# The last job of a four-layer network at its end: gate first, rotations on VectorE, shorter Newton steps, delivery tile by tile

## The chip, the cores and the metric

The kernel runs on one core of a Trainium2 chip, in one launch. The metric is the device time of that launch in microseconds (us). In this document PE is TensorE (PEld its weight loads), DVE is VectorE, ACT is ScalarE, POOL is GpSimd and SP is SyncE, which issues the DMAs. Each engine works through its own queue of instructions in order, and engines wait for each other by semaphores.

## What is computed

Input `x` has shape (4, 512, 256): B = 4 batch rows, S = 512 positions, D = 256 features, all fp32. Four layers follow each other, each added to `x` after a normalisation over the features:

```
x = x + attention_a(layernorm(x))       # 16 heads, full projections, causal softmax
x = x + gated(layernorm(x))
x = x + attention_b(layernorm(x))       # low-rank attention with rotary positions
x = x + gated(layernorm(x))
```

The change touches the gated layer alone. Its sequence axis is the batch axis: batch row l attends to rows m <= l, and each of the 512 positions is by itself. Cut to what matters:

```
x      = silu(x_prev * conv_w[:, 0] + x * conv_w[:, 1])   # x_prev: the former batch row
q      = silu(x @ Wq);  k = x @ Wk;  v = x @ Wv;  g = x @ Wg
q, k   = rotary(q), rotary(k)                             # by the batch row's number
onehot = one of two choices per head, by the larger of v @ router_w; score = its softmax value
norm   = 1 / (number of rows m <= l with the same choice)
a[m]   = (q . k[m]) * score * norm where the choices agree, times HDK**-0.5
o      = sum over m <= l of a[m] * v[m]
o      = (o - mean) / sqrt(var + eps) per head            # 16 heads of 16 numbers
out    = (silu(g) * o) @ Wout
```

## The kernel before

**Tiles and stages.** A batch row lies in four tiles `x[b][t]` of 128 positions by 256 features. The matmuls need the features on the partitions, so `norm` normalises a tile into `xn` and PE transposes it, by way of PSUM (`ps_tp`), into `xT`; even tiles are copied out by DVE, odd ones by ACT (L225). `gated` (L607 to L820) handles half of a batch row, two tiles, in one job; there are 16 jobs (two layers, four rows, two halves). It is a generator: a list of work lanes steps it, one `yield` at a time, between the pieces of the attention layers.

**The order of the work.** Nothing is rescheduled: the order in which the program emits instructions is the order of each engine's queue. During both attention layers strings of letters (`BESIDE_FULL`, `BESIDE_LOWRANK`) say which lane is stepped next: `n` the norms, `a` and `b` the two places of the gated jobs. When these strings are used up, a loop steps `"nab"` until nothing is left. Then two jobs are still open: the one before the last (row 2, second half), which has its output product and its additions to `x` ahead of it, and the last norm (row 3, second half), which hands over to the last gated job. Nothing runs beside the last job.

**One gated job, in the order of its lines.**
- Convolution: POOL multiplies the present position's `xT` with the second weight into `cx` (L619, two chunks of features); DVE adds the former row's `xT_before` times the first weight (L625). ACT takes a tanh (L630) and DVE forms the silu from it (L632); the weights hold the factor of a half.
- Projections (L641): for each of the two tiles a matmul group of 512 columns (q, k, v) and one of 272 (gate, and the difference of the two router scores `dl`). ACT copies them out of PSUM to `q`, `kv`, `gd` (L651, L652, L649).
- ACT: tanh of q (L685), of the gate (L699), of the score (`gap`, L707). DVE: choice `r` (L691), `gap` (L694), agreement `e` (L700), the silu of q (L705), `count` (L712), weights (L715 to L717), silu of the gate (L721), weights times agreement (L724).
- Rotations: `rotate` on POOL, for k and then q: four products of 128 columns (L671) and two sums (L675, L676) each.
- DVE: four products of q with the k of rows 0 to 3 and their sums per head (L734, L735), times the weights (L739).
- Weighing of the values: rows 0 and 3 by DVE, 1 and 2 by POOL (L749), with sums on DVE (L763, L769).
- ACT squares (L774); DVE sums to the variance (L777, L778) and makes a first guess of its inverse root by integer arithmetic (L783); POOL prepares `half_var` (L786) and multiplies `o` with the gate (L787); three Newton rounds of four small operations follow (L790 to L793), on POOL, in the last job on DVE.
- DVE multiplies with the root (L795), PE transposes all four blocks (L801), ACT copies them at once (L804), PE multiplies with `w_out` (L809), DVE adds to `x` (L816) tile by tile, and SP stores the tile (L1412).

**Dummy transposes.** `keep_going(count, a)` issues `count` PE transposes into a PSUM tile that nobody reads (L132), as soon as `a` is written. The last job has two such groups: 24 behind the transposes of the last norm and 70 behind L739.

In the last norm (`short`), POOL makes `rstd` by a power (L199, L200) and DVE forms both `xn` in one operation each (L211).

Of the kernel before, what the change touches and what calls it, by code (L numbers as in the profile page):

```python
# [13 lines left out]
AF = mybir.ActivationFunctionType  # L14
ALU = mybir.AluOpType
# [4 lines left out]
P = 128  # L20
# [46 lines left out]
def network(ctx: ExitStack, tc: tile.TileContext, ins: dict, out: bass.AP):  # L67
# [471 lines left out]
    def wide(tag, half, name=None, cols=None):  # L539
        tile_ = gpool.tile([P, gslots[tag]], F32, tag=f"{tag}_{half}", name=name or tag)  # L540
        return tile_[:, : cols or gslots[tag]]
# [65 lines left out]
    def gated(layer, l, xT, xT_before, half, after, newton, last=False):  # L607
# [9 lines left out]
        cx = wide("cx", half, "cx", DC * nt * P).rearrange("p (c s) -> p c s", c=DC)  # L617
        for c in range(DC):
            nc.gpsimd.tensor_scalar(  # L619
                cx[:, c, :], xT[:, c, rows], conv[:, c, 1:2], 1.0, ALU.mult, ALU.mult  # L620
            )
        yield
        if l:
            for c in range(DC):
                nc.vector.scalar_tensor_tensor(  # L625
                    cx[:, c, :], xT_before[:, c, rows], conv[:, c, 0:1], cx[:, c, :], ALU.mult, ALU.add
                )
            yield
# [8 lines left out]
        for i in range(nt):  # L637
            for lo, hi in ((0, 512), (512, NIN)):
                ps = ps_mm()
                for c in range(DC):  # L640
                    nc.tensor.matmul(  # L641
                        ps[:, : hi - lo],
                        lhsT=cx[:, c, i * P : (i + 1) * P],
                        rhs=w_in[:, c, lo:hi],
                        start=(c == 0),
                        stop=(c == DC - 1),
                    )
                if lo:
                    nc.scalar.copy(gd[:, i, :], ps[:, : DV + H])  # L649
                else:  # L650
                    nc.scalar.copy(q[:, i, :], ps[:, :DK])  # L651
                    nc.scalar.copy(kv[:, i, :], ps[:, DK:])  # L652
                yield
        gate, dl = gd[:, :, :DV], gd[:, :, DV:]
        turn_tmp = wide("cx", half, "turn")

# [22 lines left out]
        turn_k = rotate(kv[:, :, :DK]) if l else iter(())  # L679

        w0 = wide("w0", half, "thq")
        thq = w0[:, : nt * DK].rearrange("p (t k) -> p t k", t=nt)
        e = w0[:, HT * DK :][:, : B * nt * H].rearrange("p (m n) -> p m n", m=B)
        thg = wide("w1", half, "thg", nt * DV).rearrange("p (t v) -> p t v", t=nt)
        nc.scalar.activation(thq, q, AF.Tanh, scale=0.5)  # L685


        if l == 0:
            choices[half] = gpool.tile([P, B, HT * H], F32, tag=f"r_{half}", name="r")
        r = choices[half][:, l]  # L690
        nc.vector.tensor_scalar(r.rearrange("p (t h) -> p t h", t=nt), dl, -(2.0**-25), None, ALU.is_ge)  # L691
        history[layer, l, half] = kv
        gap = little("gap", nt * H)
        nc.vector.scalar_tensor_tensor(  # L694
            gap.rearrange("p (t h) -> p t h", t=nt), dl, -1.0, dl, ALU.mult, ALU.max
        )
        next(turn_k, None)
        yield
        nc.scalar.activation(thg, gate, AF.Tanh, scale=0.5)  # L699
        nc.vector.tensor_tensor(  # L700
            e[:, : l + 1], choices[half][:, : l + 1], r.unsqueeze(1).to_broadcast([P, l + 1, nt * H]), ALU.is_equal
        )
        next(turn_k, None)
        yield
        nc.vector.scalar_tensor_tensor(q, thq, 1.0, q, ALU.add, ALU.mult)  # L705

        nc.scalar.activation(gap, gap, AF.Tanh, scale=0.5)  # L707
        next(turn_k, None)
        yield
        count = little("count", nt * H)  # L710
        if l:
            nc.vector.tensor_reduce(count, e[:, : l + 1].rearrange("p m h -> p h m"), AX.X, ALU.add)  # L712
        else:
            nc.vector.tensor_copy(count, e[:, 0])
        nc.vector.reciprocal(count, count)  # L715
        nc.vector.tensor_scalar(gap, gap, 1.0, HDK**-0.5 / 4, ALU.add, ALU.mult)
        nc.vector.tensor_tensor(gap, gap, count, ALU.mult)  # L717
        turn_q = rotate(q) if l else iter(())
        next(turn_q, None)
        yield  # L720
        nc.vector.scalar_tensor_tensor(gate, thg, 1.0, gate, ALU.add, ALU.mult)  # L721
        next(turn_q, None)
        yield
        nc.vector.tensor_tensor(  # L724
            e[:, : l + 1], e[:, : l + 1], gap.unsqueeze(1).to_broadcast([P, l + 1, nt * H]), ALU.mult
        )
        next(turn_q, None)
        yield
# [11 lines left out]
        if last:  # L740
            keep_going(70, a_tile.rearrange("p m n -> p (m n)"))
# [13 lines left out]

        weigh(nc.vector, o, 0)
        if l:
            weigh(nc.gpsimd, part[1], 1)
        yield
        if l > 1:  # L760
            weigh(nc.gpsimd, part[2], 2)
# [12 lines left out]
        nc.scalar.activation(sq, og, AF.Square)  # L774
        yield
# [9 lines left out]
        )  # L785
        nc.gpsimd.tensor_scalar(half_var, var, -0.5, 1.0, ALU.mult, ALU.mult)  # L786
        nc.gpsimd.tensor_tensor(o, o, gate, ALU.mult)  # L787
        yield
        for _ in range(3):
            newton.tensor_tensor(square, root, root, ALU.mult)  # L790
            newton.tensor_tensor(square, square, half_var, ALU.mult)
            newton.tensor_scalar(square, square, 1.0, 1.5, ALU.mult, ALU.add)
            newton.tensor_tensor(root, root, square, ALU.mult)  # L793
            yield
# [11 lines left out]
        for i, t in enumerate(tiles):  # L806
            po = ps_mm()
            for c in range(DC):
                nc.tensor.matmul(  # L809
                    po[:, :D],  # L810
                    lhsT=oT[:, i, c * P : (c + 1) * P],
                    rhs=w_out[:, c, :],
                    start=(c == 0),
                    stop=(c == DC - 1),
                )
            nc.vector.tensor_tensor(x[l][t], x[l][t], po[:, :D], ALU.add)  # L816
            if after:
                after(l, t)
            yield
# [539 lines left out]
    def gated_half(layer, l, half, after=None, newton=nc.gpsimd, last=False):  # L1359

        xT = gated_in[layer][l]

        def job():
            yield from gated(layer, l, xT, gated_in[layer].get(l - 1), half, after, newton, last)
            if half:
                yield from finished(layer, l)

        return job(), half
# [10 lines left out]
    def then_gated_half(l, half):  # L1379


        def take(xT):
            gated_in[1][l] = xT

            last = (l, half) == (B - 1, 1)
            work.add(gated_half(1, l, half, store, nc.vector if last else nc.gpsimd, last))
            if last:
                keep_going(24, ident)

        short = (l, half) == (B - 1, 1)  # L1390
        return norm(l, take, tiles=HALVES[half], xT=gated_in[1].get(l), short=short)
# [23 lines left out]
    loop(attention_full(during_full, prologue))  # L1415
    while norms.jobs or work.jobs:
        beside("nab")
# [81 lines left out]
```

## Time and profile before

| | |
|---|---|
| runs, us | 1372.25, 1374.01, 1379.89; median 1374.01 |
| profiled execution, us | 1376.38 |
| its span, first to last instruction, us | 1374.7 |
| mean granted TensorE clock | 0.981 |
| instructions | 17452 |
| busy: PE, DVE, ACT, POOL | 95%, 58%, 46%, 42% of the span |
| last gated job, from the first xn to the last store issued | 1335.93 to 1372.40 us |

Times in the trace are microseconds from the start of the span. A busy share is an average over all stages; the chain of work that ended last follows the work back from the last instruction, at each step to what released it, and names engine and line. "Issue" in it is time for which the profile shows no cause. The granted clock is the share of full speed that TensorE's throttle allowed.

### The profile page before, as it was taken

The page shows a single profiled execution, that of the slowest core. Times are in us where ns is not written, and L with a number is a line of the kernel's source. Part 1 is how long each engine was busy: PE and PEld are TensorE (multiplying, and loading weights), DVE is VectorE, ACT ScalarE, POOL GpSimd, SP SyncE. Part 2 cuts the span into 40 slices and gives each one's busy share as a digit, 9 for nine tenths or more (in the row PEclk, how much of TensorE's full clock was granted, in tenths as well). Part 3 has the DMA queues.
Part 4 walks back from the last instruction along what each step waited for, and adds up shares of the span by engine and source line. Part 5 has one row for each costly group of instructions (what it writes and reads, how often), then busy time and mean ns, then how long its engine had stood idle before and what let it go on. Part 6 is the DMA issues. An engine that isn't in the chain of part 4 may idle for free.

```text
span 1374.7 us, 17452 instructions
## 1 busy us (share of the span) xinstructions
PE 1310.8 (95%) x5240; PEld 801.8 (58%) x5240; DVE 791.0 (58%) x2388; ACT 632.6 (46%) x1712; POOL 575.3 (42%) x1129
## 2 busy tenths in 40 slices
PE   9999999999999999999999888979899999999985
PEld 5555555555556656565555565647565666655554
DVE  4654445553665555755548655864646546565655
ACT  3433333343333343333343247554757666676631
POOL 3212212321125224331224745774547757675552
PEclk9999999999999999999999999989999998999998
DMA  3777765554555553554535410000000000000000
GB/s 116 223 230 213 218 201 175 161 161 123 161 167 155 161 161 108 161 165 147 164 103 176 138 32 0 1 1 1 1 9 4 5 9 1 9 1 8 1 16 8
DMA packets 88141, 133.83 MB, mean 97 GB/s; under 512 B 16112, under 2 KB 69872, under 8 KB 88048
## 3 DMA queue, kind: packets, MB, share of 16 engines
q1 hardware_dynamic: 88048, 132.72, 32.8%
q8 instruction: 42, 0.69, 0.2%
q14 instruction: 51, 0.42, 0.1%
HBM read 86.29 MB, written 46.40 MB: 97 GB/s over the span
## 4 chain that ended last, share of the span: by engine, by line
PE 80%; DVE 6%; POOL 6%; ACT 4%; issue 2%; DMA 1%; SPq 0%; POOLq 0%; DVEq 0%; ACTq 0%
PE ps_mm L338 16%; PE ps_sc L364 10%; PE ps_pz L426 10%; PE ps_mm L325 8%; PE ps_mm L448 8%; PE ps_mm L641 6%; PE ps_sc L1110 6%; PE ps_tp L1146 4%; PE ps_pz L1166 4%; PE ps_mm L1184 3%; PE ps_mm L809 2%; POOL probs L1138 1%; PE ps_mm L1084 1%; DVE ps_sc L1118 1%; ACT probs L1121 1%
## 5 line engine op out<-in xcount | busy, mean ns | idle before, releaser
L390 POOL TENSOR_SCALAR probs<-probs,sums 128x128 f32<-128x128 f32 (+3 forms) x256 | 135.8, 549 | 489.8 <-DVE sums L387 454.4
L375 ACT ACTIVATE probs<-ps_sc,sums 128x128 f32<-128x128 f32 (+3 forms) x256 | 135.0, 528 | 264.0 <-DVE sums L372 263.3
L1118 DVE CUSTOM_DVE_ANT_0 ps_sc<-ps_sc,mask_b 128x96 f32<-128x96 f32 (+15 forms) x256 | 112.3, 448 | 98.4 <-PE ps_sc L1110 90.0
L1138 POOL TENSOR_SCALAR probs<-probs,sums 128x160 f32<-128x160 f32 (+3 forms) x224 | 120.5, 556 | 111.6 <-DVE sums L1135 84.4
L1110 PE MATMUL ps_sc<-kTb,qTb 128*128 128x32 f32 (+15 forms) x512 | 159.3, 421 | 3.4 <-ACT probs L1121 3.2
L364 PE MATMUL ps_sc<-kT,qT 128*128 128x128 f32 (+3 forms) x512 | 159.2, 433 | 0.0
L1121 ACT ACTIVATE probs<-ps_sc,sums 128x160 f32<-128x160 f32 (+3 forms) x224 | 114.4, 512 | 97.0 <-DVE sums L1118 76.9
L372 DVE CUSTOM_DVE_ANT_0 ps_sc<-ps_sc,mask_a 128x128 f32<-128x128 f32 (+3 forms) x256 | 126.9, 499 | 45.7 <-PE ps_sc L364 44.8
L426 PE MATMUL ps_pz<-probsT,v 128*128 128x512 f32 (+3 forms) x512 | 148.7, 433 | 1.3 <-DMA probsT<-way 1.3
L426 PEld LDWEIGHTS ps_pz<-probsT,v 128*128 128x128 f32 x512 | 96.6, 190 | 77.8 <-issue 54.0
L439 DVE TENSOR_SCALAR zT<-ps_pz,bias 128x512 f32<-128x512 f32 x64 | 48.1, 751 | 149.1 <-PE ps_pz L426 149.0
L448 PE MATMUL ps_mm<-wo,zT 128*128 128x256 f32 x512 | 121.1, 380 | 1.3 <-ACT qTb L1018 1.3
L338 PE MATMUL ps_mm<-xT,wk 128*128 128x512 f32 x256 | 120.6, 593 | 0.4 <-ACT wvo L933 0.3
L338 PE MATMUL ps_mm<-xT,wq 128*128 128x512 f32 x256 | 120.4, 593 | 0.5 <-ACT xT L225 0.5
L325 PE MATMUL ps_mm<-wv,xT 128*128 128x512 f32 x256 | 120.3, 593 | 0.3 <-DVE xT L225 0.3
L399 DVE STREAM_TRANSPOSE squares<-probs 128x512 f32<-128x512 f32 (+3 forms) x256 | 115.1, 488 | 0.0
L1151 ACT COPY probsT<-ps_tp 128x512 f32<-128x512 f32 x160 | 92.9, 586 | 46.2 <-PE ps_tp L1146 44.7
L1146 PE MATMUL ps_tp<-ident,probs 128*128 128x128 f32 x608 | 99.7, 287 | 9.0 <-ACT probsT L1151 2.6
L364 PEld LDWEIGHTS ps_sc<-kT,qT 128*128 128x128 f32 x512 | 86.6, 191 | 34.5 <-issue 26.8
L332 ACT COPY v<-ps_mm 128x512 f32<-128x512 f32 x64 | 37.5, 586 | 148.1 <-PE ps_mm L325 148.1
L1146 PEld LDWEIGHTS ps_tp<-ident,probs 128*128 128x128 f32 x608 | 72.4, 144 | 56.2 <-issue 24.3
L448 PEld LDWEIGHTS ps_mm<-wo,zT 128*128 128x128 f32 x512 | 94.2, 191 | 18.5 <-issue 5.5
(159 smaller groups left out, 2066.4 us busy)
## 6 DMA issues: line engine op xcount, KB each, us to landing
way<-squares SPq DMA_DIRECT2D x64, 640.0 KB, 2.9
probsT<-way SPq DMA_DIRECT2D x256, 160.0 KB, 3.3
wv<-in_a_wv_dram SPq DMA_DIRECT2D x16, 512.0 KB, 5.0
wq<-in_a_wq_dram SPq DMA_DIRECT2D x32, 256.0 KB, 4.0
wk<-in_a_wk_dram SPq DMA_DIRECT2D x32, 256.0 KB, 3.9
wo<-in_a_wo_dram SPq DMA_DIRECT2D x16, 512.0 KB, 4.8
x<-in_x_dram SPq DMA_DIRECT2D x16, 128.0 KB, 3.9
out_dram<-x SPq DMA_DIRECT2D x16, 128.0 KB, 1.7
```

The costliest lines, as they stand in the source:

```text
L325: nc.tensor.matmul(pv, lhsT=xTs[b][:, c, t * P : (t + 1) * P], rhs=wv[g][:, c, :], start=(c == 0), stop=(c == DC - 1),)
L338: nc.tensor.matmul(ps, lhsT=w[u // 2][:, c, (u % 2) * DH : (u % 2 + 1) * DH], rhs=xTs[b][:, c, :], start=(c == 0), stop=(c == DC - 1),)
L364: nc.tensor.matmul(ps[:, :m], lhsT=queries[u][:, t * P : (t + 1) * P], rhs=keys[u][:, :m], start=True, stop=True,)
L372: nc.vector.tensor_tensor_reduce(ps[:, :m], ps[:, :m], mask[:, S - m :], -1.0, 3.0e38, ALU.add, ALU.min, nmax[:, t : t + 1])
L375: nc.scalar.activation(pr[:, t, :m], ps[:, :m], AF.Exp, bias=nmax[:, t : t + 1], scale=-1.0, accum_out=total[:, t : t + 1],)
L390: nc.gpsimd.tensor_scalar(pr[:, t, :m], pr[:, t, :m], inv[:, t : t + 1], 1.0, ALU.mult, ALU.mult)
L426: nc.tensor.matmul(z[:, :, k:, :], lhsT=v[:, k, j * DH : (j + 1) * DH], rhs=pT[:, :, f : f + m, :], start=(k == 0), stop=(k == NT - 1),)
L448: nc.tensor.matmul(po[:, :D], lhsT=zTs[HG * g + i][:, t].rearrange("p i b -> p (i b)"), rhs=wo[g][:, i, :], start=(i == 0), stop=(i == HG ...
L1110: nc.tensor.matmul(ps, lhsT=q[:, t % 2 * 4 + i].rearrange("p h q -> p (h q)"), rhs=kT[:, :m], start=True, stop=True,)
L1121: nc.scalar.activation(probs[i][:, :m], ps, AF.Exp, bias=nmax[:, i : i + 1], scale=-1.0, accum_out=total[:, i : i + 1],)
L1138: nc.gpsimd.tensor_scalar(probs[i][:, :m], probs[i][:, :m], inv[:, i : i + 1], 1.0, ALU.mult, ALU.mult)
L1146: nc.tensor.transpose(pt.rearrange("p (h i q) -> p h i q", h=4, i=4)[:, :, i, :], lw["probs"][t][s][i][:, k * P : (k + 1) * P], ident,)
```

## The change

It has six parts. The first two and the fourth also stand in other jobs' code, but only the first changes what they do.

1. Convolution: for rows after the first, POOL multiplies the *former* row's `xT_before` with the first weight, and DVE adds the present row. In all jobs with l > 0.
2. Behind the attention loop a line steps the lanes by `"nnnnnaaaaann"` before the `"nab"` loop starts. On the queues this has one effect: DVE's two `xn` of the last norm stand ahead of the two additions to `x` (row 2, second half), not behind them.
3. Last job only, gate first: both 272-column groups come ahead of both 512-column groups; all that depends on the gate columns alone is emitted between them; ACT takes the tanh of q tile by tile, each ahead of the copy of `kv`.
4. Last job only, rotations by DVE (`rotate_at_once`): per tensor two products of 256 columns and two sums of 128, q first, then k. The weighing of rows 1 and 2 and the product with the gate move to DVE too; the latter (`gated_o`) stands under ACT's square. POOL has no work in the last job after the convolution.
5. Last job only, Newton rounds of three operations: square, `(var * -0.5) * square`, `(square + 1.5) * root`; no `half_var`.
6. Last job only, the end tile by tile: root product, transposes and copy for 256 columns at a time. The dummy groups shrink from 24 to 18 and from 70 to 58.

The diff, cut:

```diff
-    def gated(layer, l, xT, xT_before, half, after, newton, last=False):
+    def gated(layer, l, xT, xT_before, half, after, last=False):
...
+        early, tap = (xT_before, 0) if l else (xT, 1)
         for c in range(DC):
             nc.gpsimd.tensor_scalar(
-                cx[:, c, :], xT[:, c, rows], conv[:, c, 1:2], 1.0, ALU.mult, ALU.mult
+                cx[:, c, :], early[:, c, rows], conv[:, c, tap : tap + 1], 1.0, ALU.mult, ALU.mult
             )
...
-                    cx[:, c, :], xT_before[:, c, rows], conv[:, c, 0:1], cx[:, c, :], ALU.mult, ALU.add
+                    cx[:, c, :], xT[:, c, rows], conv[:, c, 1:2], cx[:, c, :], ALU.mult, ALU.add
...
+                nc.scalar.copy(q[:, i, :], ps[:, :DK])
+                if last:
+                    nc.scalar.activation(thq[:, i, :], q[:, i, :], AF.Tanh, scale=0.5)
+                nc.scalar.copy(kv[:, i, :], ps[:, DK:])
...
+        if last:
+            parts.sort(key=lambda part: -part[1])
+            for part in parts[:nt]:
+                project(*part)
+            later = parts[nt:]
...
+        def rotate_at_once(a):
+            pairs = a.rearrange("p t (n j) -> p t n j", j=HDK // 2)
+            shape = [P, nt, 2 * H, HDK // 2]
...
+            for i in range(2):
+                nc.vector.tensor_tensor(
+                    tmp[i], pairs, rot[:, i, l - 1, :].unsqueeze(1).unsqueeze(1).to_broadcast(shape), ALU.mult
+                )
+            by_cos, by_sin = (t.rearrange("p t (a f) j -> p t a f j", f=2) for t in tmp)
+            qk = a.rearrange("p t (a f j) -> p t a f j", f=2, j=HDK // 2)
+            for f, op in ((0, ALU.subtract), (1, ALU.add)):
+                nc.vector.tensor_tensor(qk[:, :, :, f, :], by_cos[:, :, :, f, :], by_sin[:, :, :, 1 - f, :], op)
...
+        if last:
+            choose()
+            score_choice()
+            nc.scalar.activation(thg, gate, AF.Tanh, scale=0.5)
+            compare()
+            weights()
+            weigh_choices()
+            open_gate()
+            for part in later:
+                project(*part)
+            query()
+            rotate_at_once(q)
+            rotate_at_once(kv[:, :, :DK])
+            yield
...
-            keep_going(70, a_tile.rearrange("p m n -> p (m n)"))
+            keep_going(58, a_tile.rearrange("p m n -> p (m n)"))
...
+        other = nc.vector if last else nc.gpsimd
+        weigh(nc.vector, o, 0)
+        if l:
+            weigh(other, part[1], 1)
...
+        if last:
+            gated_o = wide("w1", half, "gated_o", nt * DV).rearrange("p (t v) -> p t v", t=nt)
+            nc.vector.tensor_tensor(gated_o, o, gate, ALU.mult)
...
+        if last:
+            for _ in range(3):
+                nc.vector.tensor_tensor(square, root, root, ALU.mult)
+                nc.vector.scalar_tensor_tensor(square, var, -0.5, square, ALU.mult, ALU.mult)
+                nc.vector.scalar_tensor_tensor(root, square, 1.5, root, ALU.add, ALU.mult)
+            oT = wide("w0", half, "oT", nt * DV).rearrange("p (t n) -> p t n", t=nt)
+            for i in range(nt):
+                some = slice(i * H, (i + 1) * H)
+                nc.vector.tensor_tensor(
+                    og[:, some], og[:, some], root[:, some].unsqueeze(2).to_broadcast([P, H, HDV]), ALU.mult
+                )
+                pt = ps_tp()[:, : DC * P]
+                for c in range(DC):
+                    nc.tensor.transpose(pt[:, c * P : (c + 1) * P], o[:, i, c * P : (c + 1) * P], ident)
+                nc.scalar.copy(oT[:, i, :], pt)
+            for i, t in enumerate(tiles):
+                deliver(i, t, oT)
+            return
...
-                keep_going(24, ident)
+                keep_going(18, ident)
...
+    beside("nnnnnaaaaann")
     while norms.jobs or work.jobs:
         beside("nab")
```

## The prediction

> **What bounds the kernel now.** I read the page first: busy shares, the 40 slices, then the chain of work that ended last.
>
> ```profile
> span 1374.7 us, 17452 instructions
> ...
> PE 1310.8 (95%) x5240; PEld 801.8 (58%) x5240; DVE 791.0 (58%) x2388; ACT 632.6 (46%) x1712; POOL 575.3 (42%) x1129
> ...
> PE   9999999999999999999999888979899999999985
> ```
>
> TensorE is the bound almost everywhere; only the last slice (34 us each) is thin. The diff acts there, so I next read busy time by stretch, cut where the last gated job changes stage (columns: length, then PE, weight load, DVE, ACT, POOL busy with counts, granted clock, DMA share, GB/s).
>
> ```profile
> 1334.70:1341.10 6.40, 4.21 (x32) 3.42 (x31) 3.70 (x8) 1.00 (x2) 0.94 (x2) 1.00 0.12 42
> 1341.10:1346.80 5.70, 5.62 (x16) 2.88 (x16) 0.00 (x0) 1.70 (x6) 0.00 (x0) 1.00 0.01 3
> 1346.80:1352.50 5.70, 0.00 (x0) 0.00 (x0) 3.68 (x10) 1.32 (x4) 5.46 (x12) 0.95 0.00 0
> ```
>
> The same view cut where the granted clock changes:
>
> ```profile
> 1356.50:1362.12 5.62, 5.58 (x26) 5.58 (x27) 4.93 (x5) 0.39 (x1) 2.52 (x2) 0.50 0.00 0
> 1362.12:1367.40 5.28, 4.98 (x46) 4.74 (x44) 4.39 (x15) 0.24 (x1) 1.46 (x2) 1.00 0.00 0
> ```
>
> One engine carries each stage: PE the projections, POOL the rotations (PE at zero), DVE what follows; PE's work after 1356.5 is dummy transposes, half of the time at half clock. So from 1335.6 the time is a serial chain, and the chain in order of time names its links (start, us, what):
>
> ```profile
> 1336.02 0.34 DVE xn L211
> ...
> 1337.73 0.49 POOL cx L619
> ...
> 1338.25 1.10 DVE cx L625 x2
> 1339.39 0.32 issue
> ...
> 1341.12 5.64 PE ps_mm L641 x16
> ...
> 1349.63 1.94 POOL turn L671 x4
> ...
> 1356.57 2.52 POOL part L749 x2
> ...
> 1363.85 1.26 DVE square L791
> ```
>
> The reader sees three POOL pieces that DVE waits for, and a Newton step of 1.26 that takes 0.19 in later rounds.
>
> **The change part by part.** Up to the last job the order on each engine stays; only the two convolution operands swap. That swap I cost at nothing: POOL's idle time for L619 until a transposed copy is 3.9 us in two places, 3.47 of it in the last job, so 0.44 is all it could free elsewhere. The other long DVE waits there (3.2 us at 1241) are for POOL behind its divisions, whose place is kept. SP's order does not move.
>
> *a. Norm in front, former position first.* xn now stands ahead of the two x additions of the job before. POOL's rstd power ends at 1334.26 (L200, 0.72 from 1333.54); two xn take 0.73, so they end at 1335.0 while PE is in L809 until 1335.57. The additions lie behind xn on DVE; they need PE anyway (second 1335.59 to 1336.01), so they and their stores lose nothing. The xn transposes follow L809 at 1335.59 instead of 1336.48. Four unbroken ones let ACT copy 0.72 later (row L801 to L804), at 1336.31 to 1336.69. POOL's two multiplications (0.46 apart) then lie by 1335.3 under L809, and DVE adds the present position at 1336.72: two L625 forms undisturbed start 0.39 apart and last 0.47, end 1337.59, against 1339.34. Then tanh and L632, 1.41, so the projections start at 1339.03 instead of 1341.12: **2.1**. This drops the 0.32 issue ahead of the tanh: after the square's wait (L774) ACT starts within 0.04, and most of its waits look like that. Kept, 1.8; with xn held by POOL as well, 1.3; with the copies at their earliest, 2.4.
>
> The row for xn beside POOL: L625 took 0.70 beside L619 and 0.47 alone, so +0.2, inside xn's 0.55 of slack. [...]
>
> *b. Gate first, rotations by DVE.* I count from the first projection matmul. Before, the first product L734 comes 11.42 later (1341.12 to 1352.54). After: eight 272-column matmuls (0.229 apart, first 0.33), then eight of 512 (0.43 apart), with 0.63 from the last start to the copy: the last q copy at 5.57. The gate copies end at 2.6; nine small DVE operations and the gate product (rows of 0.12 to 0.69, sum 2.5) end near 5.1, under the matmuls: free, and on the path only if they passed 6.2. ACT's extra tanhs queue ahead of kv copies, which are needed late: q copy 0.27, tanh of 128 columns 0.29 (between 0.42 for 256 and 0.22 for 32), so q is multiplied at 6.19 (0.42). Each rotation is two 256-column and two 128-column products on DVE. Rows: 0.42 for 256 (L734), 0.29 for 128 (L739); without a wait the next starts about 0.08 before the end, with one 0.035 after. That is 0.80 + 0.53 each, two rotations 2.6, first product at 9.2: **2.2**. The trace has no DVE operation on runs of four numbers. From above: POOL's rates for these same pieces (0.40 per 128, 0.455 for the sums) give 5.0 instead of 2.5, and the part −0.3; from below 2.3. I take the DVE rows: L795 with its broadcast costs the same 0.69 as a plain 512.
>
> The four products and L739 stay: 3.95.
>
> *c. All weighing by DVE.* From L739's end to the last sum: 5.21 (1356.49 to 1361.69), with L749 1.58 and L763 1.36 beside POOL. After: seven 512 operations, 0.69 to 0.70 each, three 0.61 apart unheld, the others 0.61 or 0.73: 4.6. **0.6**, ends 0 (one more held) and 0.7. Multiplying by the gate moves from POOL to DVE under ACT's square (0.63), 0.61 until the next may start: free; if the square were faster it would show.
>
> *d. Newton.* Before, L790 at 1363.54 to L795 at 1367.44: 3.90, with the 1.26 (POOL's half_var, then its gate product, 1.28 long). After: nine operations of 32 columns at 0.225 apart (row L790 to L791): 2.03. **1.9**, ends 1.7 and 1.9.
>
> *e. End by tile.* Before, L795 to the last addition: 4.17 (1367.44 to 1371.61). After: first half 0.42, +0.06 to PE, +0.45 to ACT (as L223 to L225), copy 0.37, +0.05, both tiles' matmuls 2.03: 3.4. **0.8**, ends 0.4 and 0.9. The last store follows as before.
>
> *f. Fewer dummies.* The first group (18) ends at 1338.2, before the projections need PE. The second is queued ahead of the last transposes, so its length counts. Cold pace 5.58/26 = 0.21, warm 4.98/46 = 0.11; the clock came back 5.6 after the start. 58 then take 26 cold and 32 warm, 9.1. The transposes are ready 8.9 after it: **−0.15**. Ends: never late, 0; and −0.75 for a clock 1.2 later. [...]
>
> Sum: 2.1 + 2.2 + 0.6 + 1.9 + 0.8 − 0.15 = 7.4 us. Low ends together: 1.3 − 0.3 + 0 + 1.7 + 0.4 − 0.75 = 2.3; high ends: 8.2. The profiled execution took 1376.38 (span 1374.70 and 1.68 around it), 2.37 above the median of the runs; it would be 1369.0, and the median 1374.01 − 7.4 = **1366.6**.
>
> **The rivals.**
> *Rotations dear on DVE.* If the eight operations on runs of four pay POOL's rates, 2.5 goes back: 1369.1. For it: no such DVE row. Against: L712 reads with a stride and costs what its element count costs (0.25 for 96).
> [...]
> *Body helped.* DVE waits of 6.3 us for L619 shrink because POOL no longer needs the fresh copy: the 5.4 outside the last job would give 1361.2. Against: the 0.44 above.
> *Slower.* DVE's L625 now waits for ACT's copy itself; the score evictions L1118 queued behind it feed PE. One such wait is up to an Exp and a copy, 0.69 + 0.59 = 1.3, in 11 other jobs: 14 against 7.4 won, 1380.9. It decides from 0.7 a job. Against: DVE already waited for that copy through POOL.
> *The change does not do what it says:* outside the last job "former position first" only frees POOL's wait; that is my base.
>
> **How the numbers follow.** As priced 0.68, rotations dear 0.12, dummies hold 0.12, body helped 0.05, slower 0.03. A measurement of this kernel tells about 0.5% from no change, 6.87 us, which lies just inside my 7.4. The four executions shown lie between 1372.25 and 1379.89, so a median moves by 2 to 3 us, and the first case lands beyond 0.5% two times in three: 0.68 × 0.66 + 0.05 + 0.03 from the two dear cases = 0.53; slower 0.03; within, 0.44. The range runs from the high end with scatter (1365.8 − 3) to the low ends (1374.01 − 2.3): 1362.8 to 1371.7.
>
> **What would show it.** Right: no POOL piece in the chain after the convolution; the first product some 9.2 after the first projection; Newton near 2.0; x additions 3.4 behind the root product; POOL's convolution under L809. Wrong: rotation products above 0.45 on DVE; xn above 0.5; PE's transposes released by the dummies; any shift of the projections' start that was already there before 1330.

## The result, and the profile after

The changed kernel took 1365.24 us in the median of its runs, the kernel before 1373.64 us beside it; the ratio, without the long execution named below, is 0.9928, with a 95% interval from 0.99 to 0.9955. In two further sets of runs it took 1367.53 us against 1375.99 (0.9934, 0.9912 to 0.9956) and 1367.89 us against 1374.94 (0.9942, 0.9927 to 0.9957). It is some 7 to 8 us faster, and the forecast was 1366.6 us.

The first median includes one execution of 5299.47 us, the profiled one, in which the matmuls of the costliest lines took 2.4 to 3.9 times as long (592 ns became 2304 for 128x512); the profile read here is therefore of the same program run again (1367.71 us, span 1366.0). On its page, the lines that answer those shown of before:

```profile
span 1366.0 us, 17412 instructions
...
PE 1305.0 (96%) x5222; PEld 796.2 (58%) x5222; DVE 792.0 (58%) x2397; ACT 632.2 (46%) x1714; POOL 563.7 (41%) x1113
...
PE   9999999999999999999999988979899998999986
```

POOL has 16 instructions and 11.6 us less, DVE 9 more and only 1.0 us more. Busy time by stretch, cut where the last gated job changes stage (length, then busy time and count of PE, weight load, DVE, ACT, POOL, then granted clock, DMA share, GB/s):

```profile
1331.12:1337.68 6.56, 5.36 (x29) 4.48 (x27) 3.66 (x8) 1.00 (x2) 1.09 (x2) 0.75 0.12 41
1337.68:1347.02 9.34, 5.54 (x16) 2.96 (x16) 5.21 (x18) 3.40 (x10) 0.00 (x0) 1.00 0.00 0
1347.02:1350.95 3.93, 0.00 (x0) 0.00 (x0) 3.66 (x10) 0.00 (x0) 0.00 (x0) 0.62 0.00 0
1350.95:1355.63 4.68, 4.62 (x25) 4.62 (x26) 4.54 (x9) 0.00 (x0) 0.00 (x0) 0.59 0.01 4
1355.63:1359.48 3.85, 3.77 (x35) 3.53 (x33) 3.41 (x13) 0.63 (x1) 0.00 (x0) 1.00 0.00 0
1359.48:1366.00 6.52, 2.67 (x12) 1.84 (x12) 1.60 (x4) 0.65 (x2) 0.00 (x0) 0.93 0.11 40
```

Behind the convolution POOL's column is zero, and DVE fills nearly all of three stretches in a row. The second stretch (projections to the first product) holds 18 DVE instructions, half of which now lie under PE's matmuls. The chain in order of time (start, us, what; in this kernel L903 is the earlier root product L795, L828 the output product L809, L649 the projections L641, L803 the products L734):

```profile
1328.20 0.70 DVE o L903
...
1330.40 3.30 PE ps_mm L828 x8
1333.70 0.82 PE ps_tp L223 x4
...
1335.02 0.89 DVE cx L627 x2
1335.95 0.32 issue
1336.27 0.64 ACT th L632
...
1337.68 5.55 PE ps_mm L649 x16
...
1344.42 0.77 DVE turn L687 x2
...
1345.82 0.77 DVE turn L687 x2
1346.61 0.49 DVE kv L693 x2
1347.10 0.35 DVE thq L803
...
1351.68 1.20 DVE part L818 x2
...
1357.45 0.20 DVE square L877
...
1359.48 0.44 DVE gated_o L884
...
1360.06 0.42 PE ps_tp L889 x2
...
1362.96 0.42 DVE x L835
```

No POOL piece stands in it after the convolution. The Newton pieces are 0.20 each and the wait of 1.26 is gone. One line is *worse* than before: the eight output matmuls L828 of the job before took 3.30, where the chain of other runs has 1.99. The same view, cut on the grid of 3.413 us on which the granted clock changed in these traces (1327.50 on), shows why:

```profile
1327.50:1330.90 3.40, 1.13 (x6) 0.90 (x7) 1.70 (x5) 0.58 (x1) 1.25 (x5) 1.00 0.00 0
1330.90:1334.31 3.41, 3.41 (x11) 2.75 (x11) 1.81 (x5) 0.00 (x0) 1.28 (x3) 0.50 0.11 38
```

PE was busy for 1.13 of 3.40 us, and in the next window it was granted half the clock, just while it had the output product to do. Of the nine profiled executions with the changed kernel's code in this place (the changed kernel twice, and experiments that edit other stages), four had such a window there and five not. So the table gives the undisturbed values (for section a the 7.80 of those five); the column "cold window" is what the four had. The one profile of the kernel before has no such window there; how often that kernel meets one isn't known. All times are from start to start in us, except where an end is named.

| stage (first line before / after) | before | after | gain | forecast | cold window |
|---|---|---|---|---|---|
| a. root product of the job before (L795 / L903) to first projection matmul | 9.76 | 7.80 | 1.96 | 2.1 | 9.48 or 10.47 |
| b. to the first product (L734 / L803) | 11.42 | 9.34 | 2.08 | 2.2 | |
| to the end of the weights' product (L739 / L808) | 3.95 | 3.93 | 0.02 | 0 | |
| c. to ACT's square (L774 / L858) | 5.24 | 4.68 | 0.56 | 0.6 | |
| to the end of the first guess (L783 / L872) | 1.78 | 1.78 | 0 | 0 | |
| d. to the root product (L795 / L884) | 3.94 | 2.07 | 1.87 | 1.9 | |
| e. to the last x addition (L816 / L835) | 4.17 | 3.48 | 0.69 | 0.8 | |
| f. delay of the last transposes by the dummies | | 0 | 0 | −0.15 | |
| to the end | 3.05 | 3.05 | 0 | 0 | |
| sum | 43.3 | 36.1 | 7.2 | 7.4 | 37.8 or 38.8 |

### The profile page after: what moved, and what is told of

Read it like the earlier page. It is cut to its first block, busy times and chain, and to the rows that moved or that the text cites. A ratio compares the mean times of both kernels' runs of the same rounds, so it can differ in the third digit from the quotient of the medians.

```text
span 5297.7 us, 17412 instructions
## 1 busy us (share of the span) xinstructions
PE 5279.8 (100%) x5222; PEld 2216.7 (42%) x5222; DVE 795.5 (15%) x2397; ACT 665.9 (13%) x1714; POOL 553.5 (10%) x1113
## 4 chain that ended last, share of the span: by engine, by line
PE 100%; DVE 0%; ACT 0%; issue 0%; POOL 0%; ACTq 0%; POOLq 0%; DVEq 0%
PE ps_mm L338 19%; PE ps_sc L364 12%; PE ps_pz L426 12%; PE ps_mm L325 10%; PE ps_mm L448 9%; PE ps_sc L1207 9%; PE ps_mm L649 6%; PE ps_tp L1243 5%; PE ps_pz L1263 5%; PE ps_mm L1281 4%; PE ps_mm L1181 2%; PE ps_mm L828 2%; PE ps_tp L223 1%; PE ps_sc L132 1%; PE ps_mm L1141 1%; PE ps_mm L1128 0%
## 5 line engine op out<-in xcount | busy, mean ns | idle before, releaser
L364 PE MATMUL ps_sc<-kT,qT 128*128 128x128 f32 (+3 forms) x512 | 672.6, 1552 | 0.0
L426 PE MATMUL ps_pz<-probsT,v 128*128 128x512 f32 (+3 forms) x512 | 640.5, 1524 | 0.0
L325 PE MATMUL ps_mm<-wv,xT 128*128 128x512 f32 x256 | 537.0, 2337 | 0.0
L338 PE MATMUL ps_mm<-xT,wk 128*128 128x512 f32 x256 | 529.4, 2305 | 0.0
L338 PE MATMUL ps_mm<-xT,wq 128*128 128x512 f32 x256 | 528.5, 2304 | 0.5 <-ACT xT L225 0.5
L1207 PE MATMUL ps_sc<-kTb,qTb 128*128 128x32 f32 (+15 forms) x512 | 502.9, 1164 | 0.0
L448 PE MATMUL ps_mm<-wo,zT 128*128 128x256 f32 x512 | 499.4, 1247 | 1.3 <-ACT qTb L1115 1.3
L649 PE MATMUL ps_mm<-w_in,cx 128*128 128x512 f32 (+1 forms) x256 | 333.6, 1542 | 0.0
L1207 PEld LDWEIGHTS ps_sc<-kTb,qTb 128*128 128x128 f32 x512 | 217.9, 454 | 119.8 <-issue 86.4
L1263 PE MATMUL ps_pz<-probsT,probsT 128*64 128x512 f32 (+1 forms) x320 | 228.7, 1623 | 0.0
```

The costliest lines, as they stand in the source:

```text
L325: nc.tensor.matmul(pv, lhsT=xTs[b][:, c, t * P : (t + 1) * P], rhs=wv[g][:, c, :], start=(c == 0), stop=(c == DC - 1),)
L338: nc.tensor.matmul(ps, lhsT=w[u // 2][:, c, (u % 2) * DH : (u % 2 + 1) * DH], rhs=xTs[b][:, c, :], start=(c == 0), stop=(c == DC - 1),)
L364: nc.tensor.matmul(ps[:, :m], lhsT=queries[u][:, t * P : (t + 1) * P], rhs=keys[u][:, :m], start=True, stop=True,)
L426: nc.tensor.matmul(z[:, :, k:, :], lhsT=v[:, k, j * DH : (j + 1) * DH], rhs=pT[:, :, f : f + m, :], start=(k == 0), stop=(k == NT - 1),)
L448: nc.tensor.matmul(po[:, :D], lhsT=zTs[HG * g + i][:, t].rearrange("p i b -> p (i b)"), rhs=wo[g][:, i, :], start=(i == 0), stop=(i == HG ...
L649: nc.tensor.matmul(ps[:, : hi - lo], lhsT=cx[:, c, i * P : (i + 1) * P], rhs=w_in[:, c, lo:hi], start=(c == 0), stop=(c == DC - 1),)
```

## The experiments

All edits are to the changed kernel, and are cut to the lines that decide. Sections are those of the table, taken from one profiled execution each; medians have before's runs on the same chip beside them. Five edits were executed once only: POOL's rotations took 1363.51 us, the old order of the projections 1367.65, no dummies 1370.70, 70 dummies 1368.92, POOL's weighing 1368.87. Such single times scatter too much to rank them (the first is the lowest, though one of its stretches is longer); their sections are what counts.

**The changed kernel once more, and without the front line.** The second takes out the line that steps the lanes ahead of the `"nab"` loop.

```diff
-    beside("nnnnnaaaaann")
```

> The changed kernel itself, once more, for a profile that can be laid beside the one of before. My theory (all of the gain is in the serial chain behind 1335 us, by the six parts of the prediction): the span up to the end of the job before the last (x additions of row 2) is that of before within scatter; first projection matmul 5.5 us less than before counted from the root product of the job before (before: 1341.12 - 1331.36 = 9.76; expected 7.7); first product 9.2 behind the first projection matmul (before 11.42); L808 to the last sum 4.6 (before 5.2); Newton 2.0 (before 3.9); root product to last x addition 3.4 (before 4.2); sum 7.4. Rival 1 (the body was helped by the swapped convolution): the tail sums to clearly less than the difference of the times, 8.4, and the root product of the job before starts earlier by the rest. Rival 2 (parts mis-sized): the tail alone holds 8 to 9 us, and the section times say which part.

> The changed kernel without the line that steps the lanes ahead of the loop: the two xn stand behind the two x additions again; nothing else differs. By the prediction's part a the xn transposes then wait for DVE's second addition and xn, 0.9 us later, and the first projection starts 0.7 to 0.9 us later; time up by 0.8. Rival (the front was bounded by something else, such as POOL's convolution or the copies): no more than 0.2 us between the two in the same stretch.

The first is the profile above. Its tail, with the cold window, is 37.8 us and so only 5.5 shorter than before's 43.3; the other 3.16 are there when it begins, at 1328.20 us against 1331.36. That is the sign I had set for rival 1, help in the body. Ahead of that point the clock was halved for 30.7 us here and for 41.0 in the profile of before; the next experiment takes this up.

Without the front line the median was 1370.18 us (10 runs, ratio 0.9956, 0.9938 to 0.9974). Section a was 9.02, so the line is worth 1.22 and the swap of operands the other 0.74. The line is worth more than the 0.7 to 0.9 I expected, because without it the second `xn` comes late as well. Its chain:

```profile
1328.94 2.01 PE ps_mm L828 x8
...
1330.97 0.42 DVE x L835
1331.39 0.34 DVE xn L211
...
1331.86 0.74 PE ps_tp L223 x4
```

The addition and one `xn` are on the path (0.42 + 0.34 and the hand-over), and the four transposes take 0.74 instead of the 0.45 that they take when both `xn` are there.

**The swap of operands in the last job alone.** In all other jobs POOL again multiplies the present position.

```diff
-        early, tap = (xT_before, 0) if l else (xT, 1)
+        early, tap = (xT_before, 0) if last else (xT, 1)
+        late, late_tap = (xT, 1) if last else (xT_before, 0)
...
-                    cx[:, c, :], xT[:, c, rows], conv[:, c, 1:2], cx[:, c, :], ALU.mult, ALU.add
+                    cx[:, c, :], late[:, c, rows], conv[:, c, late_tap : late_tap + 1], cx[:, c, :], ALU.mult, ALU.add
```

> The changed kernel with the convolution's operands swapped in the last job alone, all other jobs as in the kernel before. My theory (the swap is worth nothing outside the last job): same time as the changed kernel, within 1 us (0.07%). Rival (body helped): slower by the part of the gain that the tail doesn't hold, 1 to 5 us.

1368.95 us (5 runs), ratio 0.9947 (0.9927 to 0.9966), against 0.9934 (0.9912 to 0.9956) with the swap everywhere: the intervals overlap. Execution by execution this run is 1.6 us slower in the mean, with a 95% interval from about −0.5 to 3.8 (six executions against five). Neither "body helped" (5.4 us) nor "slower" (14 us) fits. A body effect of about 2 us remains possible: the tail (section a) began at 1331.36 and 1331.11 us in the two profiles with the old operands and between 1325.4 and 1330.9 in the eleven with the new ones. But that start moves with how long the clock was halved before it (fitted to the eleven, 1317.5 us plus 0.34 times that time, each within 0.9 us), and the profile of before, with 41.0 us of halved clock, lies on that line; this run, with 34.1, lies 2.0 above it. I leave it open.

**The rotations by POOL again,** with everything else as changed:

```diff
-            rotate_at_once(q)
-            rotate_at_once(kv[:, :, :DK])
+            rotate_at_once(q, nc.gpsimd)
+            rotate_at_once(kv[:, :, :DK], nc.gpsimd)
```

> The changed kernel with both rotations of the last job on POOL, in the same eight operations (two products of 256 columns and two sums of 128 for each tensor), DVE idle meanwhile. It prices the engine alone. By the rows of before (POOL 0.40 for 128 columns, 1.06 for 512, 0.455 for the sums) one rotation is about 2 x 0.62 + 2 x 0.44 = 2.1 and both 4.2 plus two hand-overs of 0.1; on DVE I put 2.6 for both: the first product 10.9 to 11.1 behind the first projection matmul against 9.2, so 1.7 to 1.9 us longer. Rival (rotations dear on DVE, runs of four numbers at POOL's rates): less than 0.3 us between the two.

From the first projection matmul to the end of the weights' product it took 8.88 + 4.55 = 13.43, against 9.34 + 3.93 = 13.27 with DVE: 0.16 longer, not 1.7 to 1.9. The timeline of POOL (start, us, line, what, count) and then of DVE:

```profile
1339.94 1.18 POOL L687 TENSOR_TENSOR turn<-q,rot 128x256 f32<-128x256 f32 x2 [10.44 <-DVE q L737]
1341.20 0.87 POOL L693 TENSOR_TENSOR q<-turn 128x128 f32<-128x128 f32 x2
1342.14 1.42 POOL L687 TENSOR_TENSOR turn<-kv,rot 128x256 f32<-128x256 f32 x2
1343.64 0.93 POOL L693 TENSOR_TENSOR kv<-turn 128x128 f32<-128x128 f32 x2
```

```profile
1342.10 0.43 DVE L803 TENSOR_TENSOR thq<-q,kv 128x256 f32<-128x256 f32 x1 [2.25 <-POOL q L693]
1342.56 0.42 DVE L804 TENSOR_REDUCE a<-thq 128x32 f32<-128x256 f32 x1
1343.01 0.83 DVE L803 TENSOR_TENSOR thq<-q,kv 128x256 f32<-128x256 f32 x1
1343.88 0.42 DVE L804 TENSOR_REDUCE a<-thq 128x32 f32<-128x256 f32 x1
1344.33 0.52 DVE L803 TENSOR_TENSOR thq<-q,kv 128x256 f32<-128x256 f32 x1
```

I had overlooked that the products with the k of rows 0 to 2 need only q. So POOL's rotation of k lies beside three of the four products. What it costs is a slower q and slower products: 0.83 and 0.52 where 0.42 is usual, while the sums keep their 0.42.

**q by DVE and k by POOL, at the same time,** k with a buffer of its own. This looks like the better split:

```diff
-            rotate_at_once(kv[:, :, :DK])
+            rotate_at_once(kv[:, :, :DK], nc.gpsimd, wide("cx", 1 - half, "turn_k"))
```

> The changed kernel with q rotated by DVE and k by POOL, in a buffer of its own, so that DVE goes on to its products of q with rows 0 to 2 meanwhile. With both on POOL (the run before this) the first product came 8.88 behind the first projection matmul and the products took 4.55, together 13.43, against 13.27 with both on DVE. Theory: what counts is that only the fourth product needs k; then DVE's share of k, 1.3, drops out and the first product comes at 8.0, and the products take 4.0 to 4.6 beside POOL: 12.0 to 12.6 together, 0.7 to 1.3 less than the changed kernel. Rival (DVE's two-input products and POOL's shut each other out, L749 beside POOL took 1.58 in place of 0.69): the products grow by POOL's 2.1 less what lies beside sums, and the whole is 13.0 or more.

9.23 + 4.04 = 13.27, the same as with DVE alone (1368.11 us, 7 runs, ratio 0.9953, 0.9938 to 0.9968). The rival was right. The timeline of POOL and then of DVE for the two rotations:

```profile
1344.69 1.37 POOL L687 TENSOR_TENSOR turn_k<-kv,rot 128x256 f32<-128x256 f32 x2 [13.01 <-ACT kv L662]
...
```

```profile
1344.81 1.53 DVE L687 TENSOR_TENSOR turn<-q,rot 128x256 f32<-128x256 f32 x2
1346.37 0.89 DVE L693 TENSOR_TENSOR q<-turn 128x128 f32<-128x128 f32 x2
```

Alone, DVE's took 0.77 and 0.49. The 1.16 that DVE lost is nearly what the rotation of k (0.77 + 0.49) would have taken on it.

**The projections in the old order,** with the gate's work behind them (gate first undone, rotations still by DVE):

```diff
-            parts.sort(key=lambda part: -part[1])
-            for part in parts[:nt]:
+            for part in parts:
                 project(*part)
-            later = parts[nt:]
+            later = []
```

> The changed kernel with the projections in the order of before (q, k, v group ahead of the gate group, tile by tile) and everything that needs the gate behind them; rotations on DVE as in the changed kernel. If gate-first is what part b won (POOL and DVE rotate both in about the same time, as the run before this shows): the gate copy of the second tile ends 6.0 behind the first projection matmul, DVE's gate operations (2.5) come on the path, then silu of q and the rotations, 3.0: first product at 11.3 to 11.8, 2.0 to 2.4 later than in the changed kernel. Rival (the gain is the engine of the rotations): no later than 9.8.

Section b took 11.87 instead of 9.34: 2.53 is lost, more than the part's whole gain and a little more than the 2.0 to 2.4 I expected. Its chain runs from the last gate copy through all small operations of the gate before DVE comes to q:

```profile
1341.26 0.34 ACT gd L657
...
1341.62 0.18 DVE r L725
...
1343.52 0.60 DVE gd L752
1344.12 0.35 DVE q L736
```

That is 2.5 us from the copy to q, as the prediction had summed for the same operations. With gate first they lie under the projections. DVE's own queue keeps these operations ahead of q in this run; q first on DVE with the old order of the projections was not run.

**No second group of dummies.**

```diff
-            keep_going(58, a_tile.rearrange("p m n -> p (m n)"))
+            keep_going(0, a_tile.rearrange("p m n -> p (m n)"))
```

> The changed kernel without the second group of dummy transposes: PE idles from the projections to the last transposes, some 15 us. It prices the clock at the end. Theory: at half clock the last four transposes and eight matmuls (two matmul groups 2.0 at full clock, transposes 0.42) take about twice as long: root product to last x addition 5.0 to 5.8 in place of 3.48, 1.5 to 2.3 us. Rival (the dummies only cost): 3.5, and no difference.

Section e grew from 3.48 to 5.37, within what I expected: the dummies earn 1.9 us. The chain shows both parts of it slower: 1.09 for the transposes and 3.65 for the products, against 0.42 on the path and 2.01 with dummies. That is about what four transposes and eight such products took at a granted clock of 0.50 in the profile of the next experiment (1.10 from 1328.55, 3.78 from 1330.37):

```profile
1361.03 1.09 PE ps_tp L889 x4
...
1362.15 3.65 PE ps_mm L828 x8
```

**The second group as long as before, 70.**

```diff
-            keep_going(58, a_tile.rearrange("p m n -> p (m n)"))
+            keep_going(70, a_tile.rearrange("p m n -> p (m n)"))
```

> The changed kernel with the second group of dummies as long as before, 70 for 58. By the prediction's part f the group is queued ahead of the last transposes and its length counts: 12 more at the warm pace of 0.11 make 1.3, the last starts 9.1 to 10.3 after the end of the weights' product a, and the first transpose, which is ready 9.1 after it, comes 0 to 1.2 late; root product to last x addition 3.5 to 4.7 instead of 3.48. By the rival the dummies' length does not matter (the transposes wait for DVE and ACT alone): 3.48.

Section e took 4.16 instead of 3.48. The chain now goes through the dummies:

```profile
1356.95 4.48 PE ps_sc L132 x41
1361.43 0.23 PE ps_tp L889 x2
```

So the length counts, as part f said. At 58 there is room in all profiled executions but one: the last dummy starts 7.8 to 9.04 us after the weights' product, and the transposes are ready 9.1 after it. In the one with 9.04, without the front line, the first transpose starts at 9.15.

**Weighing and the gate's product by POOL again.**

```diff
-        other = nc.vector if last else nc.gpsimd
+        other = nc.gpsimd
...
-            nc.vector.tensor_tensor(gated_o, o, gate, ALU.mult)
+            nc.gpsimd.tensor_tensor(gated_o, o, gate, ALU.mult)
```

> The changed kernel with rows 1 and 2 weighed by POOL again, and the gate product on POOL under the square. Part c by itself: L808's end to the square 5.2 in place of 4.68 (0.5 longer); POOL's gate product, 1.28 long, now begins with the square and ends 0.6 behind it, beside the variance sum of 0.69, which has one input: the stretch from the square to the root product stays at 3.85, or grows by up to 0.3 where Newton's two-input operations meet it. Rival (POOL's weighing lies beside DVE's for free): no difference to 4.68.

Section c took 5.36 instead of 4.68, 0.68 more, and Newton 0.06 more (2.13). In the chain POOL's two pieces and DVE's wait for them are back:

```profile
1351.52 1.50 POOL part L818
1353.02 0.02 issue
1353.04 1.54 DVE o L847
```

POOL's gate product took 1.28 and cost at most these 0.06, as it lies beside ACT's square and the variance.

**A version drawn from these runs.** Two losses are left that an edit can reach: DVE has nothing to do for 1.15 us ahead of the silu of q though the first tile's q is there, and PE's idle time ahead of L828 seems to bring the cold window. So q is finished by tile, and dummies keep PE going in the job before the last.

```diff
-            query()
-            rotate_at_once(q)
+            for i in range(nt):
+                nc.vector.scalar_tensor_tensor(q[:, i, :], thq[:, i, :], 1.0, q[:, i, :], ALU.add, ALU.mult)
+                rotate_at_once(q[:, i : i + 1, :])
             rotate_at_once(kv[:, :, :DK])
...
+        before_last = (layer, l, half) == (1, B - 2, 1)
+        if before_last:
+            keep_going(16, ident)
         for i in range(nt):
             for c in range(DC):
                 nc.tensor.transpose(
                     pt[:, (i * DC + c) * P : (i * DC + c + 1) * P], o[:, i, c * P : (c + 1) * P], ident
                 )
+        if before_last:
+            keep_going(4, ident)
```

> The changed kernel with two additions drawn from the runs so far. First: q is finished by tile (its silu, two products of 128 columns and two sums of 64 as soon as that tile's tanh is there), k still whole. In the changed kernel DVE has nothing to do for 1.14 us ahead of the silu of q, and tile 0's q is there at the start of that time; so tile 0's pieces (estimate 0.29 + 0.49 + 0.37 = 1.15) fit into it, and from the first projection matmul to the first product 8.5 to 8.8 is expected instead of 9.33. If pieces half as wide cost nearly as much as whole ones, 9.2 to 9.5. Second: 16 dummy transposes ahead of, and 4 behind, the transposes of the job before the last, where PE had nothing to do for 2.19 and 0.73 us. If half-clock windows fall on the output matmuls behind them because PE was idle there, then root product of the job before the last to first projection matmul is 7.8 here and L828's eight matmuls take 2.0, not the 9.5 to 10.5 seen in two of the profiled executions. If a half-clock window falls there all the same, or the dummies come too late, it is 8 to 10. Tail expected: 36.1 - 0.7 = 35.4. Time: 1365.5 to 1367.5 where the changed kernel has 1367.5 in the earlier call; a difference below 2 us to it is not told by the medians.

> The changed kernel itself once more, beside the two others, so that they are compared on one chip. Tail 36.1 (no half-clock window ahead of the last job) or 37.5 to 39 (one there). Time 1365 to 1369.

It took 1366.99 us (1365.86 to 1368.39, ratio 0.994, 0.9928 to 0.9952), and the changed kernel beside it 1367.89. Section a was 7.80, with a cold window at L828 in the changed kernel's profile beside it (9.48). Section b was 8.89, a little more than the 8.5 to 8.8 expected. DVE's timeline names the reason, a wait in brackets: the rotation writes into the buffer that the projections still read.

```profile
1342.92 0.49 DVE L688 TENSOR_TENSOR turn<-q,rot 128x128 f32<-128x128 f32 x2 [0.32 <-PE ps_mm L649]
```

Another run gives the rotations the other half's buffer:

```diff
-        turn_tmp = wide("cx", half, "turn")
+        turn_tmp = wide("cx", 1 - half if last else half, "turn")
```

> The kernel with q by tile and the warm-up dummies, and one change: the rotations write their products into the other half's buffer, not into the one that the projections still read. In the run before, the first product of the rotation of q's tile 0 (L688) waited 0.32 for PE's last read of that buffer. If that wait is why the first product came 8.89 after the first projection matmul and not at 8.5 to 8.8, it now comes at 8.65 to 8.75: tile 0's pieces end before tile 1's tanh, and tile 1's silu starts 6.2 after the first projection matmul instead of 6.38. If something else held it, it stays at 8.9. Root product of the job before the last to the first projection matmul: 7.8 again if the dummies keep the half-clock windows away from L828 (by chance it would be 7.8 in 5 of 9 executions), 9.5 or more if not. Tail 35.5; time 1365.5 to 1368, not to be told from the two before it by its median.

Section b was 8.73, as expected, section a 7.79, the tail 35.6. It took 1364.19 us (1363.47 to 1365.27, 6 runs) against 1377.36, a ratio of 0.991 (0.9896 to 0.9923). That is the lowest ratio of all, and the version beats both kernels by its sections. How much of the last 0.3% is its own can't be said: this kernel and the one with the wait differ by 0.1 to 0.2 us in the tail, and their ratios, from two chips, by 0.003, with intervals that don't overlap. L828 (here L830) took 1.99 again, and PE's busy time in three stretches of the grid's length around it was, in this kernel:

```profile
1323.40:1326.80 3.40, 3.31 (x24) 2.84 (x22) 0.91 (x2) 0.00 (x0) 2.17 (x9) 1.00 0.00 0
1326.80:1330.20 3.40, 2.76 (x16) 2.37 (x17) 2.18 (x8) 0.58 (x1) 1.85 (x4) 1.00 0.00 0
1330.20:1333.60 3.40, 2.70 (x24) 2.38 (x22) 2.06 (x6) 1.00 (x2) 0.19 (x1) 1.00 0.25 84
```

The least of these windows has 2.70 of busy time, where the changed kernel had 1.13. On the grid that the clock's own changes give, 0.05 to 0.08 us later, the three have 3.26, 2.84 and 2.62; the first two stand ahead of the output product. No cold window fell there in the two profiles with these dummies; without them five of nine had none either, so two of two could be chance (about three times in ten), and what speaks for the dummies is the busy time.

## Why the prediction was right, and where it was not

The time, the direction and the sum were right: 7.2 us in the undisturbed tail against 7.4. The measured difference of 7.0 to 8.5 us is of that size, but not from the tail alone. The cold window takes 1.7 or 2.7 us in four profiles of nine. Against that stands the clock in the body: the 15 ordinary executions of the changed kernel had a mean granted clock of 0.985, the 50 of the kernel before 0.981, and by the 0.72 us per 0.001 that those 50 show (last section) this goes with some 2.7 us. The tails have about the same halved time in the two profiles (11.2 and 10.2 us), so it lies mostly ahead of them. Whether the swapped operands bring it is not settled; without them outside the last job the mean was 0.984 in five executions. So it is in part luck that the medians differ by so nearly the sum. Of the signs named in the prediction all those of "right" came: no POOL piece after the convolution, the first product at 9.34, Newton 2.07, the additions at 3.48, POOL's convolution under the output product. Of those of "wrong" one came too, a shift "that was already there before 1330": 3.16 us in the profile above.

- **a, 2.1: measured 1.96, by two errors that cancel.** The step "This drops the 0.32 issue ahead of the tanh" was wrong: the pause stayed, 0.32 to 0.34, in every profiled execution. "Kept, 1.8" was too low, because the `xn` transposes came 4.03 after the root product and not at the 4.23 I had read, and DVE's addition at 5.14 and not 5.36. The two `xn` took 0.82 together beside POOL's multiplications (1.09), 0.09 more than the 0.73 of before, so less than the +0.2 was lost. The low end of 1.3 took `xn` to be held by POOL for longer; that was an estimate which no run shows: 0.09 is what it came to.
- **b, 2.2: right in size, wrong in its name.** "Rotations by DVE" took 0.38 and 0.25 per operation, 0.77 and 0.49 a pair against the 0.80 and 0.53 reckoned from DVE's plain operations, so "rotations dear on DVE" is out. But the engine of the rotations is worth only 0.16 and the order of the projections 2.53. The two don't add up to 2.08, as each was undone with the other kept. Taken one after the other, to the end of the weights' product, they do: 15.37 before; 13.43 with gate first and the new form of the rotation (four longer operations per tensor, q first) on POOL; 13.27 with it on DVE. Or: 15.37 before, 15.81 with DVE's rotations in the old order of the projections, 0.44 *longer*; 13.27 with gate first. So DVE's rotations without gate first won nothing. What the new form of the rotation is worth I did not separate.
- **c, 0.6: 0.56.** With POOL in it the section is 0.68 longer.
- **d, 1.9: 1.87,** at 0.225 from start to start, as in the row of before. No run undid it by itself.
- **e, 0.8: 0.69.** The transposes start 0.57 after the root product, against 0.48 in the sum (0.42 + 0.06). Not undone by itself either.
- **f, −0.15: 0.** The step "the transposes are ready 8.9 after it" was 0.2 short, and the clock came back 3.8 us after the group's start in the profile above, where I had 5.6. In the eleven profiles with such a group it was 3.0 to 5.6. The −0.75 of the low ends took a clock 1.2 later than the 5.6, an estimate which no run shows. So "dummies hold" is out at 58, but for the one delay of 0.05, and true at 70 (0.68).
- **Base.** "That swap I cost at nothing", outside the last job: a gain of 5.4 or a loss of 14 is excluded, a gain of some 2 us is not (interval −0.5 to 3.8), nor is the higher clock explained.
- **Range and chances.** 1362.8 to 1371.7 held all three medians, and "faster" at 0.53 against 0.44 for "within 0.5%" was about as much as could be said: the upper end of the interval, 0.9955, still lies within 0.5%. Left out of the range was the cold window of up to 2.7 us in section a. I had weighed the clock only for the dummies, not for L809, which in the profile of before ran at full clock.

## What to carry to other kernels

In a serial tail, first ask which small operations can go under the engine that is busy anyway: with the rotations on DVE, moving nine small DVE operations under the projections was worth 2.5 us; with that done, moving the rotations from POOL (1.18 and 0.87 for the pairs of q's) to DVE (0.77 and 0.49) was worth 0.16. Splitting the rotations between DVE and POOL at the same time gained nothing here (13.27 both ways): DVE's first pair took 1.53 beside POOL's instead of 0.77. Where PE idles ahead of matmuls on the path, add its busy time up by the grid on which the granted clock changes (3.413 us in these traces; half the clock followed 53 times of 53 on less than 1.4 us of busy time, never on more than 2.65) and fill the thin windows, and take the length of the filling from when the next real work is ready.

## What the runs showed of the hardware

- **Where the clock halves.** In the 13 profiled executions of ordinary length the granted clock changed only on a grid of 3.413 us, whose phase differs from run to run. From full clock, by how long PE was busy in a window: under 1.4 us the next window had half the clock 53 times of 53; 1.4 to 1.8, 30 of 53; 1.8 to 2.3, 23 of 123; 2.3 to 2.65, 6 of 103; over 2.65, never in 4671.
- **The scatter of the runs goes largely with that clock.** Over 50 executions of the kernel before, time and mean granted clock have a correlation of −0.83, and 0.001 of clock goes with 0.72 us. So 2 us of a tail drown in the body's scatter, and only sections show them.
- **DVE's and POOL's products of two tensors slowed each other.** With q rotated on DVE and k on POOL, a pair of DVE's products took 1.53 instead of 0.77 and POOL's pair 1.37 instead of 1.18. With both rotations on POOL, DVE's products beside it took 0.83 and 0.52 instead of 0.42, and its reduces stayed at 0.42.
- **A pause of 0.32 us on ACT ahead of one tanh.** Of the 16 tanhs of this line in the profile after, the last job's begins 0.32 after everything it waits for. The two others that also found ACT idle began within 0.08; ahead of the rest ACT was busy, so they can't tell. The traces of before and of the long execution have one ACT_TABLE_LOAD each, 1.28 us long at 0.79 us, so that isn't it. The pause stayed in every kernel, and its cause was not found.
